# First layer of a two-layer graph network: one-hots of two edge tiles by one two-input compare, and the first scaled loads ahead on the SyncE queue

## The chip, the core and the metric

The kernel runs on one core of one Trainium2 chip. Its engines are TensorE (PE in the profile; PEld is its weight load), VectorE (DVE), ScalarE (ACT), GpSimd (POOL) and SyncE (SP, which only issues DMAs here). Each engine works through its own instructions in the order in which the program wrote them, and engines wait for one another through semaphores. The metric is the device time of one execution in microseconds (us); lower is better.

## The reference

12500 nodes with 32 features `x`, and 200000 edges `src -> dst`, sorted by `dst`. Two layers, each with a residual:

```python
h = max(layernorm(x), 0)
# layer 0: graph convolution
out_norm = rsqrt(max(out_degree, 1)); in_norm = rsqrt(max(in_degree, 1))
agg = segment_sum((h * out_norm)[src], dst)
x = x + (agg * in_norm) @ W + b
h = max(layernorm(x), 0)
# layer 1: a message for each edge, by four linear maps
msg = concat(h[dst], h[src] - h[dst])
m = relu(relu(relu(msg @ W1 + b1) @ W2 + b2) @ W3 + b3) @ W4 + b4
x = x + segment_sum(m, dst) / max(in_degree, 1)
```

## The kernel before

**Units.** Edges are taken in tiles of 128 and chunks of four tiles (`TPC = 4`). There are 1563 tiles (`NTR`) in 391 chunks (`NCH`). The order is written out by hand (`manual_schedule`): generators are advanced in turn, and what each yields between steps decides where its instructions stand in every engine's queue.

**Stage one (0 to about 273 us): out-degrees.** DVE makes one-hots of the source's high and low digits (L352, two-input compares of fp16 numbers with `lane_g`, which is in PSUM), TensorE counts. Beside it `prepared()` makes tables for later, among them `key` (L406), `column` (recorded as `number`, L412) and the numbers `count_h` in PSUM. GpSimd gathers the raw rows of the first 48 chunks (`EARLY`) and SyncE stores them in `tab_early`; the last four (`HELD`) are stored by `keep_rows` after `scaling` has written the table `tab_hn` of scaled rows.

**Stage two (about 273 to 1300 us): layer 0.** The edges are split three ways.

- Chunks 0 to 47, *early* rows: `scale_rows(g)` loads their digits (`srow`, L760) and raw rows (`rows_back`, L763), scales them by a looked-up norm (`sturned` L766, `look` L784, `mask` L791), splits them in three bf16 terms (`rows_scaled`), makes the one-hot `hot_e` and sums them on TensorE (L813). Each unit has six steps; a new unit is begun every 12 slots and each is advanced every third slot.
- Chunks 48 to 235, *gathered* rows: one indirect DMA on GpSimd for each tile (L210, `rows<-tab_hn`, eight buffers of a chunk each), a one-hot of the destination (`hot_ahead`), and `sum_rows`, four matmuls a chunk into `ps_late`. `add_rows` adds a group of four chunks to `acc_t` (DVE L664, ACT L662), and `ps_late` has one buffer.
- The last 619 tiles (`ND`), *counted* tiles: `count_edges` forms for each tile the matrix of how many edges run from each source to each of 12 destinations, as a product of two one-hots. `onehots_of(i)` makes `oh` (128 x 1176, L833) and, for four tiles at once, `lo` (L732). Three matmuls (L897) make the counts, three ACT evictions (L899) bring them to SBUF, and after 16 tiles `multiply` (L843 and on) multiplies the counts with the whole `table` (three loads, L822).

One slot of the loop is one counted tile (`next(counting)`). The program writes `onehots_of(i + 3)` at tile i (`AHEAD_OH = 3`), and `oh` has five buffers. Also in each slot, `next(updating)` takes one step of `update_nodes`, which turns finished sums into the tables `tab_i` and `tab_j` of layer 1: `nu_aij` on ACT (L612), a store of `tab_j` (L614), then in the next step `nu_terms` on DVE (L619, L621) and a store of `tab_i`.

**Stage three (1300 us to the end): layer 1.** 1563 indirect gathers of `tab_j` on GpSimd (L210, `gj`), the four linear maps and the sums. The change does not touch it. It can begin only when the last rows of `tab_j` and `tab_i` are written.

The line of `oh` before:

```python
onehots[i] = oh = dp.tile([P, PART * WD], BF16, name="oh", bufs=5)
nc.vector.tensor_scalar(oh, column, key[:, i : i + 1], None, op0=OP.is_equal)
```

Of the kernel before, what the change touches and what calls it, by code (L numbers as in the profile page):

```python
# [8 lines left out]
F32 = mybir.dt.float32  # L9
BF16 = mybir.dt.bfloat16  # L10
# [6 lines left out]
P = 128  # L17
# [16 lines left out]
TPC = 4  # L34
# [45 lines left out]

THIRDS = [(0, 33), (33, 66), (66, PART)]
KW = 33 * WD

DPAD = (DIR + NDG * GD) * CHUNK

# [6 lines left out]
def gnn_kernel(  # L92
# [44 lines left out]
    def blocks(rows):  # L137

        return rows.rearrange("(j p) c -> p j c", p=P)
# [11 lines left out]
    rel_h = stay.tile([P, NT], F16, name="rel_h")  # L151
    rn3 = early.tile([PART, 3, P], BF16, name="rn3")
    lo_early = early.tile([P, EARLY * TPC], F32, name="lo_early")
    key = early.tile([P, ND], F32, name="key")
    column = early.tile([P, PART * WD], F16, name="number")
    pos = early.tile([WD * TD, NDG], F32, name="pos")
    bounds = early.tile([P, 4], F32, name="bounds")
    made = ctx.enter_context(ExitStack())
# [135 lines left out]
    with tc.tile_pool(name="deg", bufs=3) as hp, tc.tile_pool(  # L294
# [62 lines left out]
        def prepared():  # L357
# [36 lines left out]
            for a in range(0, ND, 512):  # L394
# [8 lines left out]
            yield  # L403
            nc.vector.tensor_reduce(bounds[:, 1:2], drel, AX.X, OP.max)
            yield
            nc.vector.scalar_tensor_tensor(  # L406
                key, hl[:, 0, DIR * TPC : NTR], float(WD), drel, op0=OP.mult, op1=OP.add)
            nc.vector.tensor_copy(lo_late, hl[:, 1, DIR * TPC : DIR * TPC + ND + 1])
            yield
            for k in range(0, PART * WD, P):  # L410
                n = min(P, PART * WD - k)
                nc.vector.tensor_scalar(column[:, k : k + n], lanes_s[:, :n], float(k), None, op0=OP.add)  # L412
            yield

            tile_i = hp.tile([P, P], I32, name="tile_i", bufs=1)
# [40 lines left out]
        def keep_rows(g, rows):  # L456

            nc.sync.dma_start(tab_early[g], rows.rearrange("p t c -> p (t c)"))
# [72 lines left out]
        while waiting or moving:  # L531
            if waiting:
                moving.append(waiting.pop(0))
            for r in list(moving):
                if next(r, moving) is moving:
                    moving.remove(r)
        for g, rows in held:
            keep_rows(g, rows)

    made.close()  # L540

# [11 lines left out]
    def update_nodes(lane, b0, n, sums_of):  # L553


        at = slice(b0, b0 + n)

        def wide(v):
            return v[:, :, None].to_broadcast([P, n, D])

        def psum(rows, width):
            return lane.bank()[:rows, :, :width]

        ps = psum(P, D + 1)
        for j in range(n):
            parts_of = sums_of(b0 + j)
            for k, (part, w) in enumerate(parts_of):
                nc.tensor.matmul(ps[:, j, :], part, w, start=(k == 0), stop=(k == len(parts_of) - 1))  # L568
        yield
        nc.vector.tensor_scalar(cnt[:, at], ps[:, :n, D], 1.0, None, op0=OP.mult)  # L570
        c = lane.tile([P, lane.width], F32, "nu_c")[:, :n]
        nc.vector.tensor_scalar(c, ps[:, :n, D], 1.0, None, op0=OP.max)
        yield
        g = lane.tile([P, lane.width], F32, "nu_g")[:, :n]
        nc.scalar.activation(g, c, AF.Sqrt)
        yield
        nc.vector.reciprocal(c, g)
        t = lane.tile([P, lane.width, D], F32, "nu_t")[:, :n]
        for j in range(n):
            nc.vector.scalar_tensor_tensor(  # L580
                x1[:, b0 + j, :], ps[:, j, :D], c[:, j : j + 1], x1[:, b0 + j, :], op0=OP.mult, op1=OP.add)
        m = lane.tile([P, lane.width], F32, "nu_m")[:, :n]
        nc.vector.tensor_reduce(m, x1[:, at, :], AX.X, OP.add)
        nc.vector.tensor_scalar(m, m, 1.0 / D, None, op0=OP.mult)
        h = lane.tile([P, lane.width, D], F32, "nu_h")[:, :n]
        nc.vector.tensor_sub(h, x1[:, at, :], wide(m))
        yield
        nc.scalar.activation(t, h, AF.Square)
        yield
        nc.vector.tensor_reduce(m, t, AX.X, OP.add)  # L590
        nc.vector.tensor_scalar(m, m, 1.0 / D, EPS, op0=OP.mult, op1=OP.add)
        yield
        nc.scalar.activation(g, m, AF.Sqrt)
        yield
        nc.vector.reciprocal(m, g)
        nc.vector.scalar_tensor_tensor(h, h, 0.0, wide(m), op0=OP.max, op1=OP.mult)
        yield
        yield
        pt = psum(D, P)
        for j in range(n):  # L600
            nc.tensor.transpose(pt[:, j, :], h[:, j, :], ident)
        yield
        ht = lane.turned[b0 // J % len(lane.turned)]
        nc.scalar.activation(ht[:D, :n], pt[:, :n], AF.Copy)
        yield
        yield
        pa = psum(P, 2 * HID)
        for j in range(n):
            nc.tensor.matmul(pa[:, j, :], ht[:, j, :], w1s, start=True, stop=True)  # L609
        yield  # L610
        aij = lane.tile([P, lane.width, 2 * HID], F32, "nu_aij")
        nc.scalar.activation(aij[:, :n], pa[:, :n], AF.Copy)  # L612
        r = P * b0
        nc.sync.dma_start(blocks(tab_j[r : r + P * n, :]), aij[:, :n, HID:])  # L614
        yield
        terms, rest = lane.tile([P, lane.width, 3 * HID], BF16, "nu_terms"), aij[:, :n, :HID]
        for k in range(3):
            part = terms[:, :n, k * HID : (k + 1) * HID]
            nc.vector.tensor_copy(part, rest)  # L619
            if k < 2:  # L620
                nc.vector.tensor_sub(rest, rest, part)  # L621
        nc.sync.dma_start(blocks(tab_i[r : r + P * n, :]), terms[:, :n])
# [78 lines left out]
    with tc.tile_pool(name="e0", bufs=8) as sp, tc.tile_pool(name="nu", bufs=1) as np_, tc.tile_pool(  # L701
# [114 lines left out]
            yield  # L816


        table = dp.tile([P, PART * D3 + P - D3], BF16, name="table")
        nc.vector.memset(table[:, PART * D3 :], 0.0)  # L820
        for a, b in THIRDS:
# [1 line left out]
                table[:, a * D3 : b * D3].rearrange("l (h c) -> l h c", c=D3), tab_hn[OFF + P * a : OFF + P * b, :].rearrange("(h l) c -> l h c", l=P))  # L823
        los, onehots, counts = {}, {}, {}
        LATE = (0, TG - 3, TG - 2)
        AHEAD_OH = 3

        def onehots_of(i):

            if i % TPC == 0:  # L830
                los[i // TPC] = one_hots(dp, lo_late[:, i : i + TPC], P, "lo", 3)
            onehots[i] = oh = dp.tile([P, PART * WD], BF16, name="oh", bufs=5)
            nc.vector.tensor_scalar(oh, column, key[:, i : i + 1], None, op0=OP.is_equal)  # L833

        def multiply(g, n):

# [37 lines left out]
        def count_edges():  # L874


            before = iter(())
            for i in range(AHEAD_OH):
                onehots_of(i)
            for i in range(ND):  # L880
                g, t = divmod(i, TG)
                if t == 0:
                    for _ in before:
                        assert False
                    if g > 0:
                        before = multiply(g - 1, TG - 3)
                    counts[g] = dp.tile([P, TG, PART, WD], BF16, name="count", bufs=2)
                if i + AHEAD_OH < ND:
                    onehots_of(i + AHEAD_OH)
                oh, lo = onehots.pop(i), los[i // TPC]  # L890
                if t not in LATE:
                    next(before, None)

                for k, (a, b) in enumerate(THIRDS):
                    ps = pp.tile([P, 512], F32, name=f"count_{k}")
                    w = (b - a) * WD
                    nc.tensor.matmul(  # L897
                        ps[:, :w], lo[:, i % TPC // 2, :, i % 2], oh[:, a * WD : b * WD], start=True, stop=True)
                    nc.scalar.activation(  # L899
                        counts[g][:, t, a:b, :].rearrange("p h d -> p (h d)"), ps[:, :w], AF.Copy)  # L900
                if t in LATE:
                    next(before, None)
                next(updating)
                yield i
            for rest in (before, multiply(NG - 1, TD - 3)):
                for _ in rest:
                    next(updating)
                    yield ND
# [5 lines left out]
        for m in range(EARLY, DIR + LAG + 1):  # L914
# [15 lines left out]
            for slot in slots:  # L930
                if next(counting, None) is None:
                    closing.append(m)
                if slot % LATER == 1:
                    while adds:
                        early, total = adds.pop()
                        sums.add(slice(0, D3), STEP * early, total)
                        added([early])
                if slot % LATER == 0:
                    advance(running)
                    later, r = divmod(slot // LATER, NEXT)  # L940
                    if r == 0 and later < EARLY:
                        running.append(scale_rows(later))
                if slot > slots[0]:
                    continue
                if EARLY <= m - 1 < DIR - 1:
                    hot_ahead(m - 1)
                if EARLY <= m - LAG < DIR - LAG:
                    sum_rows(m - LAG)
# [1 line left out]
            pass  # L950
        assert closing and not running and len(updates) <= len(lanes) and not any(missing.values())
        ending = [update_nodes(lane, *unit) for lane, unit in zip(lanes, updates)]
        for _ in range(14):
            for lane in ending:
                assert next(lane, lane) is None
    nc.scalar.activation(lanes_f, lanes_s, AF.Copy)
# [335 lines left out]
```

## Time and profile before

| | |
|---|---|
| median of 10 runs | 3279.69 us (3276.31 to 3285.43) |
| the profiled execution | 3282.34 us, of which the span from first to last instruction is 3280.6 us |
| PE busy in the span | 2538.8 us (77%) |
| DVE busy | 1559.3 us (48%) |
| ACT busy | 1532.6 us (47%) |
| POOL busy | 2437.4 us (74%) |

The profile is of one execution. A line of a *group* names the source line, the engine, the operation, output<-inputs, shapes and count, then the busy time in us, the mean duration of one in ns, and the idle time of the engine just before these instructions with what ended it. A line of *waits* names who waited for whom, the total in us, how often, and the longest. A line of the *timeline* has the start and duration in us, and in square brackets the idle time before. TensorE's ends are modelled, so its busy share overstates its load.

### The profile page before, as it was taken

To read this page: it belongs to the slowest core of one execution; us is meant where nothing else is said; L and a number is where in the kernel's file an instruction comes from. 1 tells how busy PE (TensorE), PEld (TensorE's weight loads), DVE (VectorE), ACT (ScalarE), POOL (GpSimd) and SP (SyncE) were. 2 spreads that over 40 slices of the span, in tenths; PEclk is the share of its full clock that TensorE was granted. 3 is DMA by queue.
4 is the path that set the end of the run, shared out by engine and by line. 5 is a ranking of instruction groups with operands and counts; after the bars stand their busy time and mean duration, and the time that the engine had idled before them with its cause. 6 is when DMAs were issued, how large, how long until landed. Compare 5 with 4: busy or idle time off the path is not lost.

```text
span 3280.6 us, 45395 instructions
## 1 busy us (share of the span) xinstructions
PE 2538.8 (77%) x15791; PEld 1613.6 (49%) x15791; DVE 1559.3 (48%) x4067; ACT 1532.6 (47%) x3647; POOL 2437.4 (74%) x2529
## 2 busy tenths in 40 slices
PE   3675999999988996677777777777777777777777
PEld 2573766667666775244434444434444444444333
DVE  8796877777777875122222222222222222222323
ACT  4696888888877883222222222222222222222222
POOL 7677777777766775777777777777777777777775
PEclk8587999999999997788888888888888888888898
DMA  5114122212221212222222222222222222222221
GB/s 109 31 27 89 30 38 36 36 32 39 36 39 27 41 34 58 62 65 64 64 63 63 63 66 63 63 63 63 64 65 63 63 62 63 64 65 63 63 64 34
DMA packets 242764, 180.29 MB, mean 55 GB/s; under 512 B 155496, under 2 KB 191016, under 8 KB 242528
## 3 DMA queue, kind: packets, MB, share of 16 engines
q0 software_dynamic: 80224, 73.28, 14.0%
q1 hardware_dynamic: 157436, 100.80, 11.6%
q10 hardware_dynamic: 4868, 3.23, 0.6%
q8 instruction: 128, 2.10, 0.3%
q14 instruction: 108, 0.88, 0.1%
HBM read 159.32 MB, written 17.78 MB: 54 GB/s over the span
## 4 chain that ended last, share of the span: by engine, by line
POOL 32%; issue 12%; DMA 12%; PE 7%; ACT 1%; DVE 1%; POOLq 0%; DVEq 0%; ACTq 0%
POOL gj L210 32%; DMA gj<-tab_j,src_j 11%; PE ps L1077 2%; ACT count L899 1%; PE st L843 1%; PE count L897 1%; PE p L1032 1%; PE p L1045 1%; PE p L1057 1%; PE p L1027 0%; PE p L1066 0%; PE nu_ps L609 0%; POOL rows L210 0%; PE ps_late L746 0%; PE nu_ps L568 0%
## 5 line engine op out<-in xcount | busy, mean ns | idle before, releaser
L210 POOL DMA_INDIRECT gj<-tab_j,src_j x1563 | 1481.5, 948 | 495.0 <-issue 423.0
L210 POOL DMA_INDIRECT rows<-tab_hn,src_j x752 | 759.1, 1009 | 254.3 <-issue 161.8
L899 ACT ACTIVATE count<-count 128x396 bf16<-128x396 f32 x1857 | 772.8, 512 | 114.7 <-PE count L897 107.5
L897 PE MATMUL count<-oh,lo 128*128 128x396 bf16 x1857 | 484.6, 334 | 77.5 <-DVE oh L833 36.9
L1077 PE MATMUL ps<-hot,h 128*128 128x256 f32 x1566 | 533.9, 500 | 1.8 <-ACT acc L662 1.2
L1068 DVE COPY h<-p 128x512 f32<-128x512 f32 x196 | 135.4, 691 | 774.8 <-PE p L1066 772.6
L1077 PEld LDWEIGHTS ps<-hot,h 128*128 128x128 f32 x1566 | 379.5, 255 | 184.8 <-issue 107.5
L1036 ACT ACTIVATE h<-p 128x512 f32<-128x512 f32 x196 | 117.1, 597 | 672.2 <-PE p L1032 672.2
L1025 PE MATMUL p<-gj,ident_b 128*1 128x8 bf16 x196 | 34.2, 175 | 482.0 <-DMA gj<-tab_j,src_j 466.9
L843 PE MATMUL st<-count,table 128*128 128x192 bf16 (+1 forms) x3822 | 393.2, 246 | 2.9 <-DVE acc_d L660 2.8
L843 PEld LDWEIGHTS <-table 128*128 128x128 bf16 x3822 | 320.6, 98 | 66.4 <-issue 25.3
L833 DVE TENSOR_SCALAR oh<-number,key 128x1176 bf16<-128x1176 f16 x619 | 319.4, 536 | 66.8 <-PE count L897 65.4
L664 DVE TENSOR_TENSOR acc<-acc,ps 64x64 f32<-64x64 f32 (+1 forms) x198 | 44.8, 226 | 619.1 <-PE ps L1077 568.7
L1059 ACT ACTIVATE h3t<-p,b3c 128x512 f32<-128x512 f32 x196 | 134.8, 688 | 414.6 <-PE p L1057 414.5
L1025 PEld LDWEIGHTS <-ident_b 128*1 128x1 bf16 x196 | 15.5, 79 | 628.6 <-issue 628.3
L1047 ACT ACTIVATE h<-p,b2s 128x1024 f32<-128x1024 f32 x196 | 218.0, 1112 | 123.5 <-PE p L1045 123.3
L897 PEld LDWEIGHTS <-lo 128*128 128x128 bf16 x1857 | 174.8, 99 | 162.1 <-issue 107.8
L688 DVE TENSOR_TENSOR hot<-rel_h,kept 128x512 f32<-128x512 f16 x391 | 249.9, 681 | 2.3
L1032 PE MATMUL p<-turned,ai 128*64 128x512 bf16 x1173 | 231.8, 518 | 0.0
L1045 PE MATMUL p<-h,w2s 64*128 64x512 f32 x782 | 228.3, 660 | 1.3 <-ACT h L1047 1.3
L1057 PE MATMUL p<-h,w3s 128*64 128x512 f32 x782 | 220.9, 643 | 2.1 <-ACT h3t L1059 1.9
L210 POOL DMA_INDIRECT rows_early<-tab_h,src_j x160 | 155.6, 972 | 59.9 <-issue 40.5
(256 smaller groups left out, 2858.6 us busy)
## 6 DMA issues: line engine op xcount, KB each, us to landing
row<-rel_row SPq DMA_DIRECT2D x195, 256.0 KB
gj<-tab_j,src_j POOLq DMA_INDIRECT x1563
ai<-tab_i SPq DMA_DIRECT2D x195, 96.0 KB
rows<-tab_hn,src_j POOLq DMA_INDIRECT x752
srow<-hi_row SPq DMA_DIRECT2D x48, 98.0 KB
tab_i<-nu_terms SPq DMA_DIRECT2D x23, 192.0 KB
rows_back<-tab_early SPq DMA_DIRECT2D x48, 66.0 KB
tab_j<-nu_aij SPq DMA_DIRECT2D x23, 128.0 KB
```

What stands on the lines that cost most here:

```text
L210: nc.gpsimd.indirect_dma_start(out=tile_ap, out_offset=None, in_=table, in_offset=bass.IndirectOffsetOnAxis(ap=col, axis=0))
L688: nc.vector.tensor_tensor(hot, rel_h[:, g * TPC : (g + 1) * TPC][:, :, None].to_broadcast([P, TPC, W]), lanes_f[:, None, :W].to_broadcast( ...
L833: nc.vector.tensor_scalar(oh, column, key[:, i : i + 1], None, op0=OP.is_equal)
L843: nc.tensor.matmul(ps[:, : tiles * WD], table[:, h * D3 : h * D3 + P], c[:, :tiles, h, :], start=(h == 0), stop=(h == PART - 1))
L897: nc.tensor.matmul(ps[:, :w], lo[:, i % TPC // 2, :, i % 2], oh[:, a * WD : b * WD], start=True, stop=True)
L899: nc.scalar.activation(counts[g][:, t, a:b, :].rearrange("p h d -> p (h d)"), ps[:, :w], AF.Copy)
L1032: nc.tensor.matmul(p1[k * HID : (k + 1) * HID].rearrange("p t e -> p (t e)"), v["ai"][:, k, i * HID : (i + 1) * HID], v["turned"][:, k], s ...
L1045: nc.tensor.matmul(p2[:, k], w2s[s, :], v["h1"][s, :], start=True, stop=True)
L1047: nc.scalar.activation(h2[:, :n], p2[:, :n], AF.Relu, bias=b2s)
L1057: nc.tensor.matmul(p3[k * HID : (k + 1) * HID], w3s, v["h2"][:, k], start=True, stop=True)
L1068: nc.vector.tensor_copy(h3[:, :, :rows], p4[:, :, :rows])
L1077: nc.tensor.matmul(both[: n * HID, :n, o : o + W], v["h3"][:, t, : n * HID], v["hot"][:, t, :n], start=(i == 0 and t == 0), stop=(last and ...
```

## The change

1. **`oh` by a two-input compare for two tiles.** `column` (fp16 numbers in SBUF) is dropped. `key` becomes fp16 in three copies, each shifted by a third (`KEYS = 3`, `KN = 392`), so that the numbers 0 to 391 in `count_h`, which is in PSUM already, serve all thirds. One `tensor_tensor` (`is_equal`) makes the one-hots of tiles i and i + 1, with the two tiles interleaved element by element: 128 x 2352 instead of two times 128 x 1176. A tile's one-hot is then read by TensorE with a step of two bf16 elements.
2. **Ahead and buffers.** `AHEAD_OH` goes from 3 to 4, a pair is written at each even tile, and `oh` has three buffers of a pair instead of five of a tile.
3. **The first early loads.** The two loads of `scale_rows(0)` are issued ahead of the held stores and of the three `table` loads. The held stores move out of stage one's block to just behind them.
4. **`update_nodes`** gets one more `yield` between the store of `tab_j` and `nu_terms`, and the closing loop takes 15 steps instead of 14.

```diff
+KEYS = 3
+KN = PART * WD // KEYS
...
-    key = early.tile([P, ND], F32, name="key")
-    column = early.tile([P, PART * WD], F16, name="number")
+    key = early.tile([P, KEYS, ND + ND % 2], F16, name="key")
...
+            key_f = hp.tile([P, ND], F32, name="key_f", bufs=1)
             nc.vector.scalar_tensor_tensor(
-                key, hl[:, 0, DIR * TPC : NTR], float(WD), drel, op0=OP.mult, op1=OP.add)
+                key_f, hl[:, 0, DIR * TPC : NTR], float(WD), drel, op0=OP.mult, op1=OP.add)
+            nc.vector.memset(key[:, :, ND:], 0.0)
...
-            for k in range(0, PART * WD, P):
-                n = min(P, PART * WD - k)
-                nc.vector.tensor_scalar(column[:, k : k + n], lanes_s[:, :n], float(k), None, op0=OP.add)
+            for k in range(KEYS):
+                nc.vector.tensor_scalar(key[:, k, :ND], key_f, float(-KN * k), None, op0=OP.add)
...
-        for g, rows in held:
-            keep_rows(g, rows)
...
         nc.sync.dma_start(blocks(tab_j[r : r + P * n, :]), aij[:, :n, HID:])
         yield
+        yield
         terms, rest = lane.tile([P, lane.width, 3 * HID], BF16, "nu_terms"), aij[:, :n, :HID]
...
+        running.append(scale_rows(0))
+        advance(running)
+        for g, rows in held:
+            nc.sync.dma_start(tab_early[g], rows.rearrange("p t c -> p (t c)"))
         table = dp.tile([P, PART * D3 + P - D3], BF16, name="table")
...
-        AHEAD_OH = 3
+        AHEAD_OH = 4
...
-            onehots[i] = oh = dp.tile([P, PART * WD], BF16, name="oh", bufs=5)
-            nc.vector.tensor_scalar(oh, column, key[:, i : i + 1], None, op0=OP.is_equal)
+            oh = dp.tile([P, KEYS, KN, 2], BF16, name="oh", bufs=3)
+            nc.vector.tensor_tensor(
+                oh, key[:, :, None, i : i + 2].to_broadcast([P, KEYS, KN, 2]),
+                count_h[:, None, :KN, :].to_broadcast([P, KEYS, KN, 2]), op=OP.is_equal)
+            for t in range(2):
+                onehots[i + t] = oh.rearrange("p k c t -> p (k c) t")[:, :, t]
...
-            for i in range(AHEAD_OH):
+            for i in range(0, AHEAD_OH, 2):
                 onehots_of(i)
...
-                if i + AHEAD_OH < ND:
+                if i % 2 == 0 and i + AHEAD_OH < ND:
                     onehots_of(i + AHEAD_OH)
...
-                    if r == 0 and later < EARLY:
+                    if r == 0 and 0 < later < EARLY:
                         running.append(scale_rows(later))
...
-        for _ in range(14):
+        for _ in range(15):
```

## The prediction

> **What bounds the kernel now.** I read the busy time by stage first: 0 to 273 us is stage one, 273 to 1256 the counted tiles, 1301 to the end layer 1.
>
> ```profile
> core 0: us, PE busy (x) PEld busy (x) DVE busy (x) ACT busy (x) POOL busy (x), PEclk, DMA share, GB/s
> 273.00:1256.00 983.00, 894.61 (x7688) 660.74 (x7689) 757.46 (x2494) 813.92 (x2147) 739.45 (x732) 0.97 0.23 38
> 1301.00:3281.00 1980.00, 1472.45 (x6265) 800.52 (x6265) 541.99 (x1158) 522.71 (x818) 1481.10 (x1563) 0.83 0.28 62
> ```
>
> Layer 1 is 1563 gathers at 948 ns and a 0.3 us gap each (1.25 us x 1563 = 1954 us of its 1980); the change leaves it, so its start moves the end one to one. In the counted stage no engine is full: ACT 83%, DVE 77%, and GpSimd 75% plus 0.3 us of issue before each gather. So the waits come next, with the groups of that window, and of stage one for the compare's price.
>
> ```profile
> L210 POOL DMA_INDIRECT rows<-tab_hn,src_j x732 | 740.1, 1011 | 248.2 <-issue 156.6 <-PE count L897 31.9 <-PE ps_late L746 25.1
> L833 DVE TENSOR_SCALAR oh<-number,key 128x1176 bf16<-128x1176 f16 x619 | 319.4, 536 | 66.8 <-PE count L897 65.4
> L732 DVE TENSOR_TENSOR hot<-rel_h,kept 128x512 bf16<-128x512 f16 x177 | 72.8, 411 | 0.0
> ...
> L352 DVE TENSOR_TENSOR lo<-hl,lane_g 128x2048 bf16<-128x2048 f16 x97 | 115.8, 1210 | 18.6 <-PE deg_ps L486 15.8 <-issue 2.1 <-PE turned L482 0.7
> L352 DVE TENSOR_TENSOR hi<-hl,lane_g 128x1568 bf16<-128x1568 f16 x59 | 56.6, 959 | 0.0
> ```
>
> ```profile
> ACT count L899 <- PE count L897: 107.5, 155, 7.2
> DVE oh L833 <- PE count L897: 65.4, 88, 1.7
> DVE nu_terms L619 <- ACT nu_aij L612: 49.8, 18, 3.9
> PE ps_late L746 <- ACT acc_t L662: 16.8, 16, 3.2
> ACT acc_t L662 <- DVE acc_t L664: 15.5, 12, 3.3
> PE look L813 <- DVE hot_e L732: 9.2, 7, 1.8
> ACT nu_g L593 <- DVE nu_m L591: 8.8, 3, 3.2
> ACT nu_t L588 <- DVE nu_h L586: 8.4, 5, 2.1
> ```
>
> TensorE and ACT pass each tile back and forth (the evictions start at best 381 ns apart, three a tile). DVE runs ahead (65.4 us it waits for a free `oh` buffer), but not always: rows four to eight are PE and ACT waiting for a late DVE, about 60 us in all. GpSimd is ahead too: chunk 54 was gathered 10 us before its matmuls, chunk 222 34 us, near the limit of eight buffers. Last I read the timeline at the two ends of the stage.
>
> ```profile
> 281.94 6.08 SPq L760 DMA_DIRECT2D srow<-hi_row  x1
> ...
> 292.15 0.43 DVE L766 TENSOR_SCALAR sturned<-srow,part_s 98x512 bf16<-98x512 f16 x1 [11.74 <-DMA srow<-hi_row]
> ...
> 294.07 0.49 PE L897 MATMUL count<-oh,lo 128*128 128x396 bf16 x1 [9.33 <-DVE oh L833]
> ...
> 1277.29 1.33 PE L746 MATMUL ps_late<-hot,rows 128*97 128x128 bf16 x8 [1.78 <-DVE hot L732]
> 1283.23 0.34 PE L746 MATMUL ps_late<-hot,rows 128*97 128x128 bf16 x1 [0.92 <-DMA rows<-tab_hn,src_j]
> ```
>
> At the start the first early load is issued behind the three `table` loads, DVE stands 11.74 us in front of `sturned` and TensorE 9.33. At the end TensorE waits for the last four gathers.
>
> **First loads ahead.** They go out behind the fourth `tab_hn` store, at 267.7 us instead of 281.9. SyncE waits there for the last held gathers anyhow (they go out by 272.2, and the `table` loads wait for `tab_hn` until 272.8), so two issues of 0.4 us push nothing; nobody reads the held stores before unit 44. The second unit's loads stay behind the `table` loads and landed by 292.6; its `sturned` comes about 18 tiles after 274, after 297. The 9.33 us go: -9.3. What is late next is GpSimd, 10 us ahead of TensorE at that point, so nearly all of it counts (bounds -6 and -9.3). The first pair of one-hots takes 1.37 us where one took 0.52: +0.8.
>
> **The compare.** From L352 the slope is (1210 - 959) / 480 = 0.523 ns an element (L732's 411 ns for 512, also with an inner pair and `count_h`, lies on the line), so 2352 elements are 1210 + 304 x 0.523 = 1369 ns, 685 a tile against 536. 310 of them are 424 us for 319: DVE goes from 757 to 862 us of 983, 88%. The Trainium skill (VectorE: DVE Perf Modes, "The perf-mode tier table") puts a `tensor_tensor` with any PSUM operand at one element a cycle. By it a pair would be about 2.5 us, an estimate, DVE's sum 1210 us and the kernel some 230 us slower; L352, with `lane_g` in PSUM, contradicts it, and I take the row.
>
> **What GpSimd gains.** Of 453 gathers that overlap an L833, 198 took over 1.0 us; of 123 that overlap an L352 of 2048, one did. So the gathers fall from 1011 to about 950 ns, some 45 us over 752. But GpSimd is the later one only at the end: without its last four gathers TensorE would have ended at 1278.9 instead of 1283.6. With eight buffers, chunk 235 waits for the matmuls of chunk 227 (1269.6) and lands by 1277, so -4.6, not -45.
>
> **TensorE's read in steps of two elements.** Matmuls of 128 columns start 57 ns apart with stepped `hot` (L746), 55 with contiguous `rn3` (L784): nothing to +11 us of TensorE time (6 ns x 1857) under ACT's 381; I take 0. The preparation exchanges ten instructions (1.4 us) for four: 0.
>
> **DVE's lead.** This is the large unknown; no row shows it. Before, tile i's step wrote `oh` of i + 3 into a buffer that tile i - 2 had left. Now the pair at even i reuses the buffer of i - 2 and i - 1, so DVE can start a step only when TensorE has done tile i - 1: it loses a tile of lead, 1.2 to 1.6 us. `oh` itself is safe (four tiles ahead), but `hot_e`, `acc_t` and `update_nodes` follow DVE's place. Each `scale_rows` unit puts a burst of 4 us of DVE into an even slot, now behind 1.37 instead of 0.54 us. Together 2.2 us. In quiet units `hot_e` ends 2.8 us after the unit's first count matmul and TensorE wants it at 4.5, so 0.5 us of wait appears; in some 14 of 48 it is already last. At 0.5 us each: +24. `acc_t` makes 16 of 47 groups wait; more load and less lead add 0.3 us to each: +14. Against it, `nu_terms` in the next step takes off most of 49.8 us of DVE's waits, which now cause part of the lateness: -8. Sum +30. Below: a third of the 60 us goes and nothing is added, -20. Above: the whole 2.2 us in each of 48 units less what the yield gives back, +75. I take +30, nearest to the `hot_e` rows. The quiet cycles of 12 tiles take 16.3 us when the burst starts 1.3 us ahead of its tile's matmuls, about 17 when 0.4 behind, which is that size.
>
> **Sum.** -9.3 + 0.8 - 4.6 + 30 = +17 on the profiled execution's 3282.3 us. That is 2.6 above the median, so on the median 3279.7 + 17, about 3296.
>
> **Rivals.** (1) *DVE's free time takes it, faster.* 121 us of the stage would still be idle, `nu_terms` no longer waits, and PE and ACT see no more late DVE than now: -13 to -25, 3262. For it: the 65.4 us in which DVE waits for buffers. Against it: that time is the lead that the new buffers take. It decides if `hot_e` and `acc_t` waits stay under 30 us. (2) *DVE becomes the bound.* 862 us busy and some 70 us of waits that it can't fill (`nu_c`, `acc_d`, `cnt`) leave under 5% for bursts; with the 75 us above, +62, about 3335. Against it: those waits shrink when DVE is late. (3) *Stepped reads cost TensorE.* L486, in steps of four elements, starts 98 columns every 91 ns where contiguous L482 takes 48; if steps of two did likewise, 1857 x 0.16 = 300 us, about 3500. L746 speaks against it. (4) *Nothing is seen*: the DVE cost just pays for the two ends, about 3280.
>
> **Chances.** Forecast 0.45 (3284 to 3315), (1) 0.30, (2) 0.13, (3) 0.02, (4) 0.10. The range, from the middle of (1) to just short of (2), is 3258 to 3328. A measurement here can tell about 0.2%, 6.6 us, from no change: faster than that holds (1), 0.30; within it (4) and the forecast's edge, 0.13; slower the rest, 0.57.
>
> **What would show it.** Right: `oh` near 1.37 us, 310 times; gathers in the counted stage near 950 ns; no 9 us hole at 284 to 294 us; GpSimd waiting longer for `ps_late` and `count`; PE's waits for `hot_e` and ACT's `acc_t` clearly above 26 us; the last `ps_late` matmul some 17 us later than 1283, and layer 1 as long as before. Wrong: `oh` over 2 us (the page's rule), count matmuls over 300 ns apart (rival 3), or those waits at or under 26 us with the first `gj` gather before 1290 (rival 1).

## The result and the profile after

The changed kernel takes 3360.25 us (3353.65 to 3364.43, 8 runs) where the kernel before takes 3279.48 (28 runs): ratio 1.0243, 95% interval 1.0233 to 1.0252, +81 us. The profiled execution is 3353.96 us, 71.6 above that of before. The windows view, cut at the last count matmul and at the first `gj` gather, shows where:

```profile
core 0: us, PE busy (x) PEld busy (x) DVE busy (x) ACT busy (x) POOL busy (x), PEclk, DMA share, GB/s
273.00:1329.00 1056.00, 930.10 (x7689) 670.76 (x7690) 876.58 (x2181) 817.16 (x2146) 693.31 (x732) 0.96 0.21 35
1374.00:3352.00 1978.00, 1478.38 (x6265) 802.83 (x6265) 540.54 (x1157) 522.93 (x818) 1480.77 (x1563) 0.83 0.28 63
```

The counted stage is 73 us longer, layer 1 is as long as before. DVE works 119 us more, GpSimd 46 less, and ACT, which does the same work, works 817 us for 814: ACT's idle time grows by 70 of these 73 us. The groups of that stage:

```profile
L211 POOL DMA_INDIRECT rows<-tab_hn,src_j x732 | 693.3, 947 | 367.4 <-issue 168.8 <-PE ps_late L747 140.9 <-PE count L906 39.8
...
L838 DVE TENSOR_TENSOR oh<-key,kept 128x2352 bf16<-128x2352 f16 x310 | 426.1, 1375 | 133.1 <-PE count L906 132.3
```

The pair costs 1375 ns and the gathers 947. DVE stands 132 us in front of an `oh` buffer, twice as long as before, though it has more to do. Who waits for DVE stands in the list of waits of the same stretch (total us, times, longest):

```profile
POOL rows L211 <- PE ps_late L747: 140.9, 79, 4.5
DVE oh L838 <- PE count L906: 132.3, 122, 3.7
...
ACT acc_e L663 <- DVE acc_e L665: 44.0, 32, 3.2
...
ACT acc_t L663 <- DVE acc_t L665: 32.6, 12, 4.4
PE ps_late L747 <- ACT acc_t L663: 28.3, 17, 4.1
...
PE look L814 <- DVE hot_e L733: 23.8, 26, 2.0
...
PE st L852 <- DVE acc_d L661: 8.9, 6, 2.2
```

Of the rows that wait for DVE, the one that grew most is `acc_e`, which the prediction never named. In the same list of the kernel before it is

```profile
ACT acc_e L662 <- DVE acc_e L664: 5.4, 10, 2.1
```

`sums.add` splits each sum of early rows between the two engines (DVE adds to the columns that hold a sum already, ACT copies the fresh ones), and ACT's part waits until DVE has done its own. The timeline shows what it looks like:

```profile
704.22 0.41 DVE L733 TENSOR_TENSOR lo<-lo_late,kept 128x512 bf16<-128x512 f16 x1
704.35 1.41 PE L852 MATMUL st<-count,table 128*128 128x192 bf16 x15 [1.54 <-DVE acc_d L661]
704.55 1.37 DVE L838 TENSOR_TENSOR oh<-key,kept 128x2352 bf16<-128x2352 f16 x1
...
705.84 0.24 DVE L665 TENSOR_TENSOR acc_e<-acc_e,look 97x96 f32<-97x96 f32 x1
...
706.11 0.20 ACT L663 ACTIVATE acc_e<-look 97x32 f32<-97x32 f32 x1 [2.52 <-DVE acc_e L665]
...
706.21 1.26 ACT L908 ACTIVATE count<-count 128x396 bf16<-128x396 f32 x3
```

DVE is late. Its `acc_e` step of 0.24 us stands behind a `lo` of 0.41 us and a pair of 1.37 us, ACT stands 2.52 us in front of its own 0.20 us part, and the next evictions of counts stand behind that. Ten microseconds later DVE itself is held:

```profile
715.18 1.38 DVE L838 TENSOR_TENSOR oh<-key,kept 128x2352 bf16<-128x2352 f16 x1 [1.64 <-PE count L906]
...
716.59 0.35 DVE L792 SCALAR_TENSOR_TENSOR mask<-lanes_s,lo_early,look 128x128 f32<-128x128 f32 x1
...
720.31 0.41 DVE L733 TENSOR_TENSOR hot_e<-rel_h,kept 128x512 bf16<-128x512 f16 x1
...
720.78 0.39 PE L814 MATMUL look<-hot_e,rows_scaled 128*97 128x128 bf16 x4 [0.52 <-DVE hot_e L733]
```

It idles 1.64 us for a buffer, then makes a pair that nobody needs for four tiles, then the burst of a unit, and TensorE waits for the end of that burst. So DVE waits for TensorE and TensorE for DVE, in turn.

### The profile page after: what moved, and what is told of

It is laid out like the page before. It is cut to its first block, busy times and chain, and to the rows that moved or that the text cites. A ratio compares the mean times of both kernels' runs of the same rounds, so it can differ in the third digit from the quotient of the medians.

```text
span 3352.2 us, 44996 instructions
## 1 busy us (share of the span) xinstructions
PE 2581.5 (77%) x15791; PEld 1627.7 (49%) x15791; DVE 1678.1 (50%) x3752; ACT 1536.6 (46%) x3647; POOL 2391.3 (71%) x2529
## 4 chain that ended last, share of the span: by engine, by line
POOL 30%; DMA 12%; issue 11%; PE 9%; ACT 2%; DVE 1%; POOLq 0%; DVEq 0%; ACTq 0%
POOL gj L211 30%; DMA gj<-tab_j,src_j 12%; PE ps L1086 2%; ACT count L908 1%; PE st L852 1%; PE count L906 1%; PE p L1054 1%; PE p L1041 1%; PE p L1066 1%; PE p L1036 1%; PE p L1075 0%; DVE oh L838 0%; PE st L877 0%; PE ps_late L747 0%; PE nu_ps L609 0%
## 5 line engine op out<-in xcount | busy, mean ns | idle before, releaser
L211 POOL DMA_INDIRECT rows<-tab_hn,src_j x752 | 712.4, 947 | 373.5 <-issue 174.0
L906 PE MATMUL count<-oh,lo 128*128 128x396 bf16 x1857 | 504.8, 345 | 77.3 <-ACT count L908 37.1
L838 DVE TENSOR_TENSOR oh<-key,kept 128x2352 bf16<-128x2352 f16 x310 | 426.1, 1375 | 133.1 <-PE count L906 132.3
L1034 PEld LDWEIGHTS <-ident_b 128*1 128x1 bf16 x196 | 15.5, 79 | 621.2 <-issue 620.6
```

The costliest lines, as they stand in the source:

```text
L211: nc.gpsimd.indirect_dma_start(out=tile_ap, out_offset=None, in_=table, in_offset=bass.IndirectOffsetOnAxis(ap=col, axis=0))
L838: nc.vector.tensor_tensor(oh, key[:, :, None, i : i + 2].to_broadcast([P, KEYS, KN, 2]), count_h[:, None, :KN, :].to_broadcast([P, KEYS, K ...
L906: nc.tensor.matmul(ps[:, :w], lo[:, i % TPC // 2, :, i % 2], oh[:, a * WD : b * WD], start=True, stop=True)
```

## The experiments

Three theories. **LEAD**: the new buffers let DVE start a step only when tile i - 1 is done, and each short step behind it is late. **PRICE**: DVE's 95 us of extra compare time (310 x 1375 ns less 619 x 536 ns) do it. **READ**: TensorE's stepped read does it.

There were six groups of runs, each on another chip and against the kernel before on that chip. In four of them the kernel before itself takes 3978 to 4018 us, and no difference over 0.4% shows, so they are told last. In the other two it takes 3279 and 3282.

How far each kernel is behind the kernel before (us, profiled executions; start of the first count matmul of a tile, then the first `gj` gather):

| tile | 12 | 100 | 200 | 300 | 400 | 500 | 618 | `gj` |
|---|---|---|---|---|---|---|---|---|
| changed (first profile) | -6.7 | 8.5 | 19.6 | 30.0 | 43.5 | 59.5 | 72.9 | 72.6 |
| changed again (after_2) | -6.1 | 8.4 | 21.4 | 39.2 | 51.9 | 68.2 | 80.5 | 80.2 |
| two ahead (a_ahead2_3) | -7.5 | -5.2 | -4.7 | -3.8 | -1.8 | 2.6 | 2.9 | 2.7 |
| contiguous read (a_contig_2) | -4.9 | 10.6 | 27.5 | 44.8 | 58.1 | 70.7 | 82.8 | 82.4 |
| clears, four buffers (b_price_bufs4_2) | 0.7 | 8.4 | 18.5 | 24.2 | 30.3 | 33.2 | 40.2 | 39.4 |
| loads, step, six buffers (b_loads_yield_bufs6_2) | -8.7 | -6.4 | -12.3 | -15.1 | -17.6 | -18.3 | -20.4 | -17.8 |

The loads gain at once what they gain, and the loss then grows with every tile, about 0.13 us each. The stage by engine, from 273 us to the last count matmul (windows and waits, us; the idle time is the stretch less ACT's busy time):

| | tile that `oh` waits for | stretch | DVE busy | ACT busy | ACT idle | ACT waits for DVE's `acc` steps |
|---|---|---|---|---|---|---|
| before | i - 2 | 983 | 757 | 814 | 169 | 22.5 |
| changed | i - 1 | 1056 | 877 | 817 | 239 | 79.5 |
| a_ahead2_3 | i - 3 | 987 | 871 | 818 | 169 | 25.7 |
| a_contig_2 | i - 1 | 1066 | 876 | 817 | 249 | 79.0 |
| b_price_bufs4_2 | i - 1 | 1024 | 812 | 816 | 208 | 41.0 |
| b_loads_yield_bufs6_2 | i - 3 | 963 | 758 | 813 | 150 | 19.8 |

From before to changed, 57 of the 70 us of ACT's extra idle time stand in front of its `acc` steps (79.5 less 22.5).

**The changed kernel again**, for comparison. 

> The changed kernel unchanged, as the point of comparison for the other runs of this group. Where the kernel before takes some 3280 us again, 3350 to 3365 by every theory. Where it takes some 3980 to 4010, as in the two groups before this one, TensorE stands still for other reasons (the tile period there is 2.0 us for 1.59): LEAD and PRICE expect the loss to shrink to under 40 us, since DVE catches up in these stretches; READ expects 9 ns x 1857 = 17 us there too.

3362.44 us, ratio 1.0246 (1.0229 to 1.0263).

**Pairs two tiles ahead.** At even i the pair for i + 2 goes into the buffer of i - 4 and i - 3; price and stepped read stay. The constant moves one thing more: `lo`, the compare that serves four tiles (0.41 us), is written with the pair of its first tile, so it goes two slots on as well.

```diff
-        AHEAD_OH = 4
+        AHEAD_OH = 2
```

> The changed kernel with pairs written two tiles ahead instead of four, against the changed kernel in the same group. LEAD: it takes back 40 to 80 us where the kernel before takes 3280 (3280 to 3320), and all that is lost where it takes 3980. PRICE or READ: within 10 us of the changed kernel.

3285.32 us, ratio to before 1.0018 (1.0008 to 1.0027): 77 us less than the changed kernel in the same group. Window and waits:

```profile
273.00:1260.00 987.00, 907.42 (x7701) 660.42 (x7702) 871.21 (x2185) 817.77 (x2149) 695.07 (x733) 0.98 0.24 38
```

```profile
PE count L906 <- DVE oh L838: 40.9, 17, 25.4
...
ACT acc_t L663 <- DVE acc_t L665: 17.4, 9, 4.6
...
DVE oh L838 <- PE count L906: 8.9, 14, 1.2
...
ACT acc_e L663 <- DVE acc_e L665: 7.7, 12, 1.9
PE look L814 <- DVE hot_e L733: 6.8, 7, 1.7
```

DVE is busy 871 of 987 us (88%), with the same pairs, and stands 9 us in front of a buffer instead of 132; the waits for `acc_e` and `hot_e` are back near what they were in the kernel before (5.4 and 9.2). So PRICE alone is refuted, and the loss needs the tie of DVE to TensorE, as LEAD has it; that the tie alone would do it is not shown by this run. The price is seen too: from tile 12 to 618 this kernel loses 10 us, and TensorE waits 15.5 us for one-hots (40.9 less the 25.4 at the start of the stage), for which two tiles ahead is sometimes too late.

The place of `lo` isn't parted from the tie here: in the changed kernel it stands right in front of the pair ahead of 47 of the 48 bursts and of 47 `acc_e` steps, with two ahead in front of one of them in all. In 35 and 4 of these DVE then waited for the buffer anyhow, which leaves 55 times 0.41 us, an estimate of at most 23 of the 77 us for it. A slower group speaks for the tie too: there four pair buffers (a_bufs4) leave `lo` where the changed kernel has it and lift the tie, and ACT's waits `acc_e` and `acc_t` are 14.2 us in sum, 12.8 with two ahead (a_ahead2) and 27.6 with the tie (a_contig).

**Contiguous read.** TensorE reads 1176 columns in a row, so what it counts is a mix of two tiles; the work and the waits stay as they are. 

> The changed kernel with TensorE reading each one-hot as 1176 contiguous columns of the pair instead of every second one; what it counts is a mix of the two tiles. READ: it takes back what the step costs, 17 us if all of it stands on the path, count matmuls 166 ns apart instead of 175. LEAD and PRICE: at most 17 us of the loss goes, 3340 to 3360 where the kernel before takes 3280.

```diff
-                onehots[i + t] = oh.rearrange("p k c t -> p (k c) t")[:, :, t]
+                onehots[i + t] = oh.rearrange("p k c t -> p (k c t)")[:, t * PART * WD : (t + 1) * PART * WD]
```

3363.23 us, ratio 1.0256 (1.0239 to 1.0273): as the changed kernel. The closest count matmuls start 166 ns apart again instead of 175, and nothing comes of it. That fits ACT's evictions, of which a tile has three and which start 370 ns apart at best. READ is refuted. The group of count matmuls here, then in the changed kernel of the same group:

```profile
L906 PE MATMUL count<-oh,lo 128*128 128x396 bf16 x1857 | 497.0, 341 | 83.9 <-ACT count L908 38.7 <-DVE oh L838 25.4 <-DVE look L800 0.4
```

```profile
L906 PE MATMUL count<-oh,lo 128*128 128x396 bf16 x1857 | 506.2, 347 | 78.9 <-ACT count L908 38.6 <-DVE oh L838 25.3 <-DVE look L800 0.4
```

**Old compare with the tie and the extra work.** The kernel before, four `oh` buffers and a clear behind each one-hot. 

> The kernel before with a small clear of some 150 ns behind each one-hot and with four oh buffers instead of five: the price and the tie of the change without its pairs and its stepped read. LEAD and PRICE together: 3330 to 3365 where the kernel before takes 3280. If under 3310 there, the rest of the loss lies in the block of 1.37 us or in the stepped read.

```diff
+        pad = dp.tile([P, 110], F32, name="pad", bufs=1)
...
-            onehots[i] = oh = dp.tile([P, PART * WD], BF16, name="oh", bufs=5)
+            onehots[i] = oh = dp.tile([P, PART * WD], BF16, name="oh", bufs=4)
             nc.vector.tensor_scalar(oh, column, key[:, i : i + 1], None, op0=OP.is_equal)
+            nc.vector.memset(pad, 0.0)
```

3319.83 us, ratio 1.012 (1.0103 to 1.0137), +41: half of the loss, short of what was expected. Its waits (`oh` is L834 here):

```profile
DVE oh L834 <- PE count L899: 146.5, 196, 3.2
...
ACT acc_t L662 <- DVE acc_t L664: 24.7, 14, 3.4
...
ACT acc_e L662 <- DVE acc_e L664: 13.2, 19, 2.3
...
PE look L813 <- DVE hot_e L732: 10.4, 8, 1.9
```

DVE stands as long in front of its buffers as in the changed kernel, but in 196 short waits, and ACT and TensorE wait half as long or less for `acc_e` and `hot_e`. Each clear takes 150 ns as meant, but some 30 ns of it overlap the compare ahead and other rows are a little shorter, so DVE is busy only 812 us, not 877: this run has 55 of the 119 us of extra work. What remains to the changed kernel is that other half of the work, the pair as one block of 1.37 us, the place of `lo` and the extra step; no run parts these.

**No pairs, early loads, the extra step, six buffers.** If the lead is what counts, more of it should gain. 

> The kernel before with the first early loads ahead, the extra step of update_nodes and six oh buffers instead of five, one-hots by the old compare. Where the kernel before takes some 3280: LEAD 3245 to 3268 (a tile more of lead, and no wait for nu_aij in DVE's way, beyond the loads' -9); PRICE 3268 to 3273, the loads alone. Where it takes some 3980: within 20 us of it, nothing told apart.

```diff
-        for g, rows in held:
-            keep_rows(g, rows)
...
         nc.sync.dma_start(blocks(tab_j[r : r + P * n, :]), aij[:, :n, HID:])
         yield
+        yield
...
+        running.append(scale_rows(0))
+        advance(running)
+        for g, rows in held:
+            nc.sync.dma_start(tab_early[g], rows.rearrange("p t c -> p (t c)"))
...
-            onehots[i] = oh = dp.tile([P, PART * WD], BF16, name="oh", bufs=5)
+            onehots[i] = oh = dp.tile([P, PART * WD], BF16, name="oh", bufs=6)
...
-                    if r == 0 and later < EARLY:
+                    if r == 0 and 0 < later < EARLY:
...
-        for _ in range(14):
+        for _ in range(15):
```

3271.48 us against 3281.92, ratio 0.9969 (0.9957 to 0.9982): 10.4 us faster than before and so some 90 faster than the change, the one version that beats both. By what was expected this lies in PRICE's range, the loads alone, and 3.5 us above LEAD's, so the time doesn't show that more lead gains. One profile, of the fastest of its six runs, has more: 8.7 us are won at the start and 11.7 along the stage; the tail gives 2.6 back and layer 1 took 3.7 longer. Whether the step or the sixth buffer won the 11.7 isn't parted. Its waits:

```profile
DVE nu_terms L618 <- ACT nu_aij L610: 37.4, 16, 4.1
...
DVE oh L836 <- PE count L900: 26.3, 50, 1.2
...
PE ps_late L745 <- DMA rows<-tab_hn,src_j: 12.7, 10, 3.2
...
PE look L812 <- DVE hot_e L731: 6.1, 6, 1.7
```

DVE's free time is no longer spent on `oh` buffers (26 for 65 us) but on work that isn't there yet, and gathers begin to be what TensorE waits for.

**The four other groups.** First what was expected of them.

Four buffers of a pair (`oh` `bufs=4`, the pair then waits for tile i - 3; room made by `rows` with four buffers instead of eight and one `raw_sq`): 

> The changed kernel with four pair buffers of one-hots instead of three; to make room, the gathered rows have four chunk buffers instead of eight and one square tile instead of two. Theory LEAD (the pair buffers let VectorE start a step only when TensorE has done the tile before, and everything that follows VectorE's place comes late): two tiles of lead come back, so most of the loss goes, 3275 to 3300 us, with VectorE's 133 us of waiting for TensorE at the one-hots cut to less than half and the waits for hot_e, acc_t and acc_e with it. Theory PRICE (VectorE's 95 us more of work and its 1.37 us blocks make it late whatever the buffers): 3340 to 3360 us. Theory READ (TensorE reads the one-hots in steps of two elements, 175 ns a matmul for 166): 3360 us, no change.

Two tiles ahead, twice: 

> The changed kernel with its three pair buffers, but AHEAD_OH 2 instead of 4: the pair of tiles i + 2 and i + 3 is written at i into the buffer of i - 4 and i - 3. VectorE may be two tiles further ahead of TensorE at the same memory; a one-hot itself is due two tiles later instead of four. LEAD: hot_e, acc_t and acc_e come early again, 3280 to 3310 us, unless the one-hots themselves come late. PRICE: 3350 us or more, with TensorE waiting for one-hots. READ: 3360 us.

> The changed kernel with its pairs written two tiles ahead instead of four, so that a pair reuses a buffer that TensorE left three tiles before: DVE's place is free again, the price and the stepped read stay. LEAD: most of the loss goes, 3275 to 3310. PRICE or READ: 3345 to 3365 as the changed kernel. If two tiles are too few for a pair, count waits for oh appear and it is slower than 3360.

The kernel before with four buffers, the tie alone: 

> The kernel before with four one-tile buffers of one-hots instead of five: at tile i the one-hot of i + 3 goes into the buffer of i - 1, so VectorE is tied to TensorE as closely as in the changed kernel, at the old price of 536 ns a tile. LEAD: 40 to 70 us slower than before, 3320 to 3350 us. PRICE and READ: 3280 us, no change, since neither the price nor the layout is touched.

Contiguous read: 

> The changed kernel, but TensorE reads contiguous halves of the pair's one-hots instead of every second element (the counts are then of mixed tiles; every instruction, size and wait is the same otherwise). READ: the count matmuls return from 175 to 166 ns apart and the time falls by 16 us or more (1857 x 9 ns, and more if ScalarE is starved by it), to 3345 us or below. LEAD and PRICE: at most 10 us less, 3350 to 3360 us.

The same, again and once more: 

> The kernel before with four oh buffers of a tile instead of five: DVE can write a step's one-hot only when TensorE has done tile i - 1, as in the change, but at the old price. [...] LEAD alone (the tie to TensorE is most of the loss): 3279 + 50 to 80, 3330 to 3360, DVE's wait for oh near 130 us. PRICE alone (DVE's extra work is most of it): within 10 us of 3279. Both needed: +10 to +35, 3290 to 3315.

> The kernel before with four oh buffers of a tile instead of five: the tie alone, at the old price. Both together (small clears and four buffers) gave 3320, +41. LEAD: the tie alone gives most of that, 3300 to 3320. PRICE: within 8 us of 3279. If the two only count together: 3282 to 3300.

> The kernel before with four oh buffers of a tile instead of five: the tie alone, at the old price. Where the kernel before takes some 3280: LEAD alone 3300 to 3320, most of the +41 of tie and work together; PRICE within 8 us of 3279; if the two only count together 3282 to 3300. Where it takes some 3980: nothing told apart, as twice before.

The kernel before with the clears alone: 

> The kernel before with one small clear of 110 fp32 columns (some 150 ns by the rows of such clears) behind each of the 619 one-hots: DVE's work rises by some 93 us as in the change, its place against TensorE stays free by five buffers. PRICE alone: +50 to +80, 3330 to 3360. LEAD alone: within 10 us of 3279. Both needed: +15 to +40, 3295 to 3320.

Again: 

> The kernel before with a small clear of some 150 ns behind each one-hot and its five oh buffers: the extra DVE work alone. PRICE: 3305 to 3320. LEAD: within 10 us of 3279, since the pairs two tiles ahead with the same extra work lost only 6 us in all, with a start that gains 9.

Clears and four buffers: 

> Both of the former: the small clears and four oh buffers of a tile. LEAD or PRICE alone: as the one of the two that loses. Both needed: +60 to +90, 3340 to 3370, more than the sum of the two single runs. If it stays under +40 the remaining loss of the change lies in what it has besides: the pair as one block of 1.37 us, TensorE's stepped read (9 ns longer between count matmuls, 1857 of them, 17 us at most), or the extra step.

Part 3 of the change alone: 

> The kernel before with the first early loads ahead alone (part 3 of the change). By the prediction's term -9.3 (bounds -6 and -9.3): 3270 to 3273. A rival, that GpSimd is late next and takes it back: within 3 us of 3279.

Loads, step and six buffers: 

> The kernel before with the first early loads ahead, the extra step of update_nodes and six oh buffers instead of five, one-hots by the old compare. LEAD: a further tile of lead and the waits for nu_aij out of DVE's way gain beyond the loads: 3245 to 3268. PRICE: no more than the loads, 3268 to 3273.

| run | ratio to the kernel before (95%) |
|---|---|
| a_bufs4, a_ahead2 | 0.9996 (0.9976 to 1.0017), 0.9981 (0.9961 to 1.0002) |
| b_bufs4, a_contig | 0.9984 (0.9960 to 1.0009), 1.0035 (1.0013 to 1.0056) |
| b_bufs4_2, b_price | 1.0003 (0.9976 to 1.0030), 0.9976 (0.9953 to 1.0000) |
| b_price_bufs4, a_ahead2_2 | 0.9971 (0.9947 to 0.9994), 0.9986 (0.9956 to 1.0016) |
| b_bufs4_3, b_price_2 | 0.9996 (0.9973 to 1.0019), 1.0009 (0.9990 to 1.0028) |
| b_loads, b_loads_yield_bufs6 | 1.0012 (0.9984 to 1.0039), 1.0036 (1.0013 to 1.0060) |
| b_bufs4_4 | 0.9976 (0.9954 to 0.9999) |

Here a tile takes 2.0 us instead of 1.59, and even b_price_bufs4, 1.2% slower elsewhere, loses nothing. That fits LEAD (a tie to TensorE costs nothing where TensorE is held up anyway), but a_contig, which has the tie, is 0.35% slower, and b_loads_yield_bufs6, which is faster than before elsewhere, is 0.36% slower, so it isn't a proof. Expectations that give times near 3280 are neither met nor missed by these runs. The changed kernel itself was not run there. So three questions stay open: what the tie costs at the old price, what the extra work costs with five buffers, and what the first loads give alone.

## Why the prediction was wrong

The direction was right, the size was not: +17 forecast, +81 measured, outside the range. By its steps:

- **First loads, -9.3 and +0.8.** Right in kind, slightly too good: the stage is 6.7 us ahead at tile 12 (8.7 with the old compare, in the last experiment). SyncE shows the new order, one issue right behind the other:

```profile
267.58 0.69 SPq L761 DMA_DIRECT2D srow<-hi_row  x1
268.32 0.37 SPq L764 DMA_DIRECT2D rows_back<-tab_early  x1
268.88 3.59 SPq L823 DMA_DIRECT2D tab_early<-rows_early  x4
272.64 9.78 SPq L827 DMA_DIRECT2D table<-tab_hn  x3
```

- **The compare.** 1369 ns forecast from the L352 rows, 1375 measured. The Trainium skill (VectorE: DVE Perf Modes, "The perf-mode tier table") would have made it some 2.5 us, by the estimate in the prediction; the run contradicts the table's PSUM entry for a two-input operation.
- **GpSimd.** The gathers fell to 947 ns as forecast, and gained almost nothing: from the last count matmul to the last `ps_late` matmul it is 26.9 us, 27.4 before, so -4.6 was wrong. The faster gathers only waited longer for a free buffer (141 us for `ps_late`, 25 before). The working asked whether chunk 235 waits for chunk 227; the last wait came earlier, at chunk 230 for chunk 222, and the 24 gathers from there on need 24 x 1.25 = 30 us. Before, GpSimd's last wait of that kind lay 80 gathers from the end. Timeline of GpSimd before, then after:

```profile
1177.28 1.14 POOL L210 DMA_INDIRECT rows<-tab_hn,src_j  x1 [1.25 <-PE ps_late L746]
```

```profile
1324.21 0.94 POOL L211 DMA_INDIRECT rows<-tab_hn,src_j  x1 [1.27 <-PE ps_late L747]
```

- **Stepped read, 0.** Right: it costs 9 ns a matmul (6 in the working), and the contiguous run shows that nothing of it reaches the time. The 381 ns between evictions are their median, not the best; the best is 370.
- **DVE's lead, +30: the step that failed.** From tile 12 to 618 the changed kernel lost 79.6 us in one profile and 86.6 in the other, above even the upper bound of 75. The mechanism was the one named, and the loss of lead too: the burst of a unit starts at the median 1.24 us behind its tile's first count matmul, where it was 0.08 ahead, and with two tiles ahead it is 0.28 behind. That is a shift of 1.3 us where the working had 2.2; what was too small is the price put on it, in four places. First, ACT's `acc_e` was left out: 5.4 us before looked like nothing, and became 44.0, the largest growth of a wait for DVE; `hot_e`, priced at +24, grew by 14.6, and `acc_t`, priced at +14, by 18.4 (with the 1.6 and 2.9 us of its rows for `acc`). Second, 0.5 us a unit came from the quiet cycles. Over all stretches of 12 tiles, the shortest went from 15.8 to 15.4 us, but the quartiles from 17.4, 18.6 and 20.1 to 19.0, 20.1 and 21.7: 1.5 to 1.6 us in a typical cycle. Third, the relief of -8 by the extra step: the waits for `nu_aij` did vanish, but only because DVE is now held in front of `oh` for longer than it ever waited there (with two tiles ahead 21.8 us of them are back). Fourth, the burst was put behind the pair alone; with `AHEAD_OH = 4` `lo` stands in the same slot, so up to 0.41 us more stand ahead of it (nothing where DVE waits for the buffer anyhow). The upper bound has a slip of its own: the whole 2.2 us in 48 units are 106, and to come to 75 the yield has to give back 31, where the sum has 8.
- **The rivals.** (1) fell with its own condition: `hot_e` and `acc_t` waits are 56 us, not under 30. (2) came nearest in size (its +62 on the median is 3342, not the 3335 written there), but its mechanism is refuted: at 88% busy DVE does the stage in 987 us when its buffers let it. (3) is refuted by the contiguous read, (4) by the time.

The sum with the measured terms, for the profiled execution: -6.7 to tile 12, +79.6 to the end of the counts, -0.3 to the first `gj` gather, and -1.0 for the rest, is 71.6.

## What to carry to other kernels

For an engine that feeds another through a ring of buffers, work out for each write which consumer step it waits for, and remember that everything behind it in the engine's queue waits as well: looking further ahead than the buffers bear (four tiles ahead with six tiles of buffers) delays the short steps that others need soon, and one constant (two ahead) took back 77 of the 83 us that the change cost in that group. When an engine loses lead, list every row in which someone waits for that engine, the small ones above all, and take the price from the middle of the cycles, not from the quiet ones. The longer block cost little by itself: with the same pairs written two ahead the kernel is 6 us behind the one before. And a changed look-ahead moves every step that goes by the same tile number, here `lo`.

## What the runs showed of the hardware

- A moving operand read in steps of two bf16 elements lengthens the closest spacing of matmuls of 396 columns from 166 to 175 ns.
- With the compare that reads PSUM, the 752 gathers of rows take 947 to 949 ns in the mean; with the old one from SBUF alone 983 (with the small clears) to 1013.
- The same program takes 3279 to 3282 us in two of the groups and 3978 to 4018 in the other four. Each group had its own chip, so the chip and the moment aren't told apart. The single instructions are hardly longer there (a count matmul 328 ns at the median in b_price, 330 in the kernel before), but the three of a tile start 328 ns apart at the median instead of 172, the granted clock is 0.81 instead of 0.865 in the mean, and engines stand between instructions for nothing the profile shows. Layer 1's gathers, first in the kernel before at 3282 us, then in b_price at 3977 (from 1650 us on; `remote` is a release for which the profile has no instruction):

```profile
L210 POOL DMA_INDIRECT gj<-tab_j,src_j x1563 | 1481.5, 948 | 495.0 <-issue 423.0 <-DMA gj<-tab_j,src_j 47.6 <-DMA tab_i<-nu_terms 18.9
```

```profile
L210 POOL DMA_INDIRECT gj<-tab_j,src_j x1560 | 1473.7, 945 | 827.8 <-issue 463.4 <-remote 248.2 <-PE p L1029 40.0
```

What holds them up there stays open.
